# A projected block and a group's row transposes move into the attention's third place, in a decoder layer

## The chip, the cores and the metric

The kernel runs on one core of one Trainium2 chip. The metric is the device time in microseconds (us) of one execution, the median of several runs. Engines are named as in the profile: PE (TensorE, the matmuls), PEld (its weight loads), DVE (VectorE), ACT (ScalarE), POOL (GpSimd) and SP (the queue that issues most transfers).

## The reference

Four sequences of 512 rows and 512 columns go through one decoder layer, in float32:

```python
x = x + attn(layernorm(x))           # causal, 16 heads of 32, with q, k, v, o weights and biases
x = x + xattn(layernorm(x), ctx)     # no weights; q = layernorm(x), k = v = ctx; masked scores are -10000
x = x + relu(h @ W_up.T) @ W_down.T + sum(softmax(top2(h @ W_gate.T))) * (h @ W_expert)   # h = layernorm(x)
```

Both attentions subtract the largest score of each row before the exponential. In the cross attention a masked score is -10000 and not minus infinity, so rows whose largest score lies far below take part with their masked columns too; the kernel adds these from sums over the columns behind the diagonal.

## The kernel before

The loop over the four sequences `b` runs in program order; the engines' orders are the order in which the Python code records the instructions (a manual schedule for PE, DVE, ACT and POOL). Semaphores and PSUM buffers are set by the framework. PSUM holds four tiles of tag "ps", each a pair of 512-column banks (`pair`); a new tile takes a buffer that was freed, and its first matmul waits for the engine that read it last.

An attention has 16 heads in four groups `g` of four (HG = 4, 32 rows each) and works in two stages.

- `with_maxima` (L905) goes through ten units of scores, two row blocks or one at a time: `maxima` computes scores of 128 queries by up to 512 keys (tiles `sm_`, four heads side by side in row tiles of 32), ACT copies them to SBUF (`s_`), POOL masks the diagonal (L312), DVE takes the negated row maxima (`nm_`, L324). Between the units PE gets full-array matmuls from a list of `steps` (`fill`), spread evenly by `due`: projections of this or a neighbouring sequence. When a group's maxima are complete, `split` (L341) writes each as three bfloat16 parts into `parts0` or `parts1`. `rows` (L352) transposes these on PE with four 128x128 matmuls into rows `mrow_`, for groups 0 and 1 within this stage.
- `attend` (L954) goes through ten units of transposed scores (`scores`, tiles `sc_`, two pairs each, the first for two heads and the second for the other two). A second set of matmuls (L416) adds the negated maxima from `mrow_`. ACT takes the exponential (`pt_`, or `sum_` for a group's first block), POOL masks the diagonal (L447), and `values` multiplies with v two units later (`pv_`, column tiles of 32, L482). Row sums are made partly by DVE, which adds the later blocks onto `sum_` (`add_up`, L552), and one matmul with ones at the end (`summed`, L558).

Before, groups 2 and 3 of a self-attention get their row transposes together behind unit 3 of `attend` (`mt_s_both`, eight transposes, counted from unit 0). In a cross-attention group 2's stand at the end of `with_maxima`, group 3's behind unit 3, with group 2's broadcast of the maxima over heads (`masked_sums`, L374); group 3's broadcast stands behind unit 7.

The steps that fill `with_maxima` are the query and key projections (`query_key`, ACT adds the bias), the value projection (`value`, DVE adds the bias, L685), `up` (ACT takes the relu), `gate`, `down` (DVE adds to x, L843) and `expert` (DVE weighs and adds, L867). Each projects one block of 128 rows or columns with four matmuls; two blocks share one PSUM pair, which is read once both are done:

```python
if t % 2 == 0:
    made[0] = pair(f"pm_v{b}_{t}")
yield from project(made[0][:, t % 2, :], e.xn_t, wv_sb, t)
if t % 2 == 1:
    nc.vector.tensor_tensor(e.v[:, t - 1 : t + 1, :], made[0], ..., ALU.add)
```

The attentions are named s0 to s3 and c0 to c3. The fill of s0 is the rest of its query and key projections and its value projection; that of s1 and s2 the previous sequence's up, gate and down; that of s3 four experts and two ups; that of c1 query and key of the next sequence and four experts.

Of the kernel before, what the change touches and what calls it, by code (L numbers as in the profile page):

```python
# [18 lines left out]
P = 128  # L19
# [7 lines left out]
def decoder_layer(  # L27
# [37 lines left out]
    def pair(name):  # L65

        return ps.tile([P, 2, S], F32, tag="ps", name=name)


    def load_x(b):  # L70
        xb = act.tile([P, NT, D], F32, tag="x", name=f"x_{b}", bufs=2)
# [194 lines left out]
    class Attention:  # L266
# [82 lines left out]
            nc.vector.tensor_copy(pt[:, :, :, 1], rest)  # L349
            nc.vector.tensor_tensor(pt[:, :, :, 2], rest, pt[:, :, :, 1], ALU.subtract)  # L350

        def rows(self, g, both=None, half=0):  # L352


            if both is None:
                tp = ps.tile([P, NT, P], BF16, tag="ps", name=f"mt_{self.name}_{g}")
            else:
                bank = both[:, 0, :].bitcast(BF16)
                tp = bank[:, half * S : (half + 1) * S].rearrange("p (i q) -> p i q", q=P)
            for i in range(NT):  # L360
                nc.tensor.transpose(tp[:, i, :], parts[g % 2][:, i, :], identb)
            self.mrow[g] = work.tile(
                [P, S], BF16, tag="mrow", name=f"mrow_{self.name}_{g}", bufs=4
            )

            def copy(engine=nc.vector.tensor_copy):
                engine(self.mrow[g], tp.rearrange("p i q -> p (i q)"))

            return [copy]

        def masked_sums(self, g, both=None):

            bc = (pair(f"mb_{self.name}_{g}") if both is None else both)[:, 1, :]
            nc.tensor.matmul(bc, lhsT=same, rhs=self.mrow[g], start=True, stop=True)  # L374
            return g, bc

        def masked(self, g, bc):
# [298 lines left out]
    def value(e):  # L676
        b, made = e.b, {}
        e.v = act.tile([P, NT, D], F32, tag="v", name=f"v_{b}")

        def one(t):  # L680
            if t % 2 == 0:
                made[0] = pair(f"pm_v{b}_{t}")
            yield from project(made[0][:, t % 2, :], e.xn_t, wv_sb, t)
            if t % 2 == 1:
                nc.vector.tensor_tensor(  # L685
                    e.v[:, t - 1 : t + 1, :],
                    made[0],
                    bv_sb.unsqueeze(1).to_broadcast([P, 2, D]),
                    ALU.add,
                )  # L690

        return [(lambda t=t: one(t)) for t in range(NT)]

    def context(e):

# [82 lines left out]
    def ffn(e):  # L778
        b, f_t, made = e.b, e.f_t, {}

        def up(f):
            if f == 0:
                made["h"] = act.tile(
                    [P, NC, S], F32, tag="o_t" if b != B - 2 else "f_t", name=f"hT_{b}"
                )
            if f % 2 == 0:
                made["u"] = pair(f"pm_u{b}_{f}")
            yield from project_t(made["u"][:, f % 2, :], wup_sb, f_t, f)
            if f % 2 == 1:
                nc.scalar.activation(made["h"][:, f - 1 : f + 1, :], made["u"], AF.Relu)  # L790
# [41 lines left out]
            nc.vector.tensor_reduce(made["rw"], ew, axis=AX.X, op=ALU.add)  # L832

        def down(t):
            if t % 2 == 0:
                made["d"] = pair(f"pm_d{b}_{t}")
            yield from project(made["d"][:, t % 2, :], made["h"], wdown_sb, t)
            if t == NT - 1 and b == B - 2:
                for n in range(2):
                    aside(f"d{b}_{n}", t - 1 + n, made["d"][:, n, :])  # L840
            elif t % 2 == 1:
                both = e.x[:, t - 1 : t + 1, :]
                nc.vector.tensor_tensor(both, made["d"], both, ALU.add)  # L843

        def expert(t):
            if b == B - 1 and t == NT - 1:
                yield from expert_parts(t)
                return
            last = b == B - 1 and t == NT - 2
            if t % 2 == 0:  # L850
                made["e"] = pair(f"pm_e{b}_{t}")
            yield from project(made["e"][:, t % 2, :], f_t, wexp_sb, t)
            for n in (0,) if last else (0, 1) if t % 2 == 1 else ():
                u = t - t % 2 + n
                weigh(u, made["e"][:, n, :], slice(0, D), nc.sync)
# [46 lines left out]
            yield from step() or ()  # L902
            yield

    def with_maxima(steps, a, first=0, norms=()):  # L905


        norms = list(norms)
        run(steps[:first])
        fill = matmuls(steps[first:])  # L910
        total = sum(1 if step.__name__ in ("share", "gate") else NC for step in steps[first:])

        units = []
        for g in range(0, NC, 2):
            units += [[(g, 1), (g + 1, 1)]]
            units += [u for k in (g, g + 1) for u in ([(k, 2), (k, 0)], [(k, NT - 1)])]

        lead = 2 if first else 0
        for _ in range(lead):
            next(fill)  # L920
        done, due, jobs, late = lead, float(lead), [], {3: NC - 1}
        todo = []
        for n, pieces in enumerate(units):
            new = a.maxima(pieces)
            if todo:
                todo.pop()(nc.gpsimd)
            if norms and n % 2 == 0:
                new.append(norms.pop(0))
            due += (total - lead) / len(units)

            count = round(due) - done
            for k in range(count):
                next(fill, None)
                done += 1
                if k == min(1, count - 1) and n in (5, 7):
                    jobs = a.rows((n - 5) // 2) + jobs
                if k == min(1, count - 1) and a.cross and n in (6, 8):
                    todo.append(a.masked(*a.masked_sums((n - 6) // 2)))
                if n == len(units) - 1 and k == count - (2 if count > 4 else 1):
                    if total >= 2 * len(units):  # L940
                        if a.cross:
                            a.rows(2)[0](nc.scalar.copy)
                    else:
                        late = {3: 2, 5: NC - 1}
                run(jobs[:1])
                jobs = jobs[1:]
            run(jobs)
            jobs = new
        for _ in fill:
            pass  # L950
        run(jobs)
        return late

    def attend(a, late):  # L954


        units = []
        for g in range(0, NC, 2):
            units += [[(g, 0)], [(g, 3), (g, 1)], [(g, 2), (g + 1, 2)]]
            units += [[(g + 1, 0)], [(g + 1, 3), (g + 1, 1)]]  # L960
        waiting, held, todo = [], [], []

        def values():
            made = waiting.pop(0)
            a.values(made)

            if len(made) > 1 and made[0][1] == 2:
                held.append(made[1:])
            elif waiting and waiting[0][0][1] > 0:
                if made[0][1] == 0 and held:  # L970
                    a.add_up(held.pop())
                a.add_up(waiting[0] if waiting[0][0][1] == 3 else waiting[0][:1])
                if waiting[0][0][1] == 2 and waiting[0][1][0] == a.joined:
                    a.join(waiting[0][1], waiting[1][0])

        for n, pieces in enumerate(units):
            waiting.append(a.scores(pieces))
            if n in late:
                two = a.cross and late[n] == NC - 1
                together = not a.cross and len(late) == 1  # L980
                both = pair(f"mt_{a.name}_both") if two or together else None
                copies = a.rows(2, both, 1) if together else []
                copies += a.rows(late[n], both)

                more = [a.masked_sums(2, both)] if two else []
                for copy in copies:
                    copy(nc.scalar.copy)
                todo.extend(a.masked(*each) for each in more)
            if a.cross and n == 7:
                todo.append(a.masked(*a.masked_sums(3)))  # L990
            if n in (4 if a.joined is None else 6, 6, 9) and todo:
                todo.pop(0)()
            if n in (3, 4) and put_off:
                put_off.pop(0)()
            if len(waiting) > 2:
                values()
        while waiting:
            values()

    with tc.manual_schedule(engines=BY_HAND):  # L1000
# [11 lines left out]
        for b in range(B):  # L1012
# [2 lines left out]
            norms, turns = [], []  # L1015
            if more:
                after, norms, turns = norm_in(b + 1)
            late = with_maxima(between_self, sa, skip, norms)
            if b == B - 1:
                e.x = load_x(b)  # L1020
            attend(sa, late)
            if b > 0:
                add_bias(e)
            made = out_projection(e, sa, context(e) + turns)
# [4 lines left out]
            norm_cross(e, made, 2)  # L1029
            ca = Attention(e.cq_t, e.ck_t, e.cv, True, f"c{b}")  # L1030
            ca.e, ca.out = e, e.beh_t
            late = with_maxima(steps[3:], ca)
            if b + 2 < B:
                after.x = load_x(b + 1)
            attend(ca, late)
            if more:
                cvs[b + 1] = load_cv(b + 1)
            filler = value(after) if more else ahead
# [73 lines left out]
```

## Time and profile before

| | |
|---|---|
| median of 3 runs | 804.19 us (804.04 to 805.84) |
| profiled execution, span from first to last instruction | 803.7 us |
| mean granted TensorE clock in it | 0.998 |
| PE busy, matmuls | 794.0 us, 99%, 5588 records |
| DVE busy | 565.9 us, 70% |
| ACT busy | 395.2 us, 49% |
| POOL busy | 339.6 us, 42% |

The span of the profiled execution lies 0.5 us below the median of the runs; what lies around the span is not in the profile. A float32 matmul stands as two records in it, a bfloat16 matmul as one. "Idle before" names what ended an engine's idle time. A matmul's end is modelled, so that a short wait can stand within busy time; starts of instructions are better compared than their durations.

### The profile page before, as it was taken

What the parts mean: (1) busy time and instruction counts of PE and PEld (TensorE: products, weight loads), DVE (VectorE), ACT (ScalarE), POOL (GpSimd) and SP (SyncE); (2) the same over time, 40 slices, a digit from 0 to 9 for tenths busy, and PEclk for the clock granted to TensorE, in tenths of its full rate; (3) what the DMA queues carried; (4) which work ended last, traced back from release to release, by engine and by line L of the source; (5) the groups of instructions that cost most, each with busy time, mean ns of one, the idle gap of its engine ahead of it and who ended that gap; (6) DMA issues with size and microseconds to landing.
All of it is one profiled execution on the core that took longest, in us unless ns stands there. A gap on an engine that the chain in (4) does not pass through costs nothing.

```text
span 803.7 us, 13927 instructions
## 1 busy us (share of the span) xinstructions
PE 794.0 (99%) x5588; PEld 378.9 (47%) x5592; DVE 565.9 (70%) x963; ACT 395.2 (49%) x448; POOL 339.6 (42%) x523
## 2 busy tenths in 40 slices
PE   8999999999999999999999999999999999999998
PEld 6444454444444454444544455444444444444544
DVE  2378855889679854678867786588959766988512
ACT  2457516871456615567055742687156833674110
POOL 3434612564234732257332482256423652475100
PEclk9999999999999999999999999999999999999999
DMA  9710000001010000021100000000102000000101
GB/s 301 275 28 1 2 1 1 2 27 54 1 27 2 2 0 1 2 78 55 53 14 14 1 2 0 1 1 2 53 28 80 2 1 1 1 2 1 53 1 52
DMA packets 15282, 24.51 MB, mean 30 GB/s; under 512 B 2033, under 2 KB 5361, under 8 KB 15217
## 3 DMA queue, kind: packets, MB, share of 16 engines
q1 hardware_dynamic: 14496, 22.96, 8.6%
q8 instruction: 44, 0.72, 0.4%
q10 hardware_dynamic: 720, 0.66, 0.2%
q14 instruction: 22, 0.17, 0.1%
HBM read 19.42 MB, written 4.19 MB: 29 GB/s over the span
## 4 chain that ended last, share of the span: by engine, by line
PE 95%; ACT 2%; issue 1%; DMA 1%; DVE 0%; ACTq 0%
PE pm_qk L241 14%; PE pm_d L229 7%; PE pm_u L241 7%; PE pm_v L229 7%; PE pm_o L725 7%; PE pm_e L229 7%; PE pv_c L482 6%; PE pv_s L482 6%; PE sm_c L293 6%; PE sm_s L293 6%; PE sc_s L405 5%; PE sc_c L405 5%; PE sc_s L416 1%; PE sc_c L416 1%; PE tp_a L255 1%
## 5 line engine op out<-in xcount | busy, mean ns | idle before, releaser
L324 DVE TENSOR_REDUCE nm_s<-s_s 128x2 f32<-128x1024 f32 (+3 forms) x128 | 96.9, 810 | 34.7 <-POOL s_s L312 34.7
L324 DVE TENSOR_REDUCE nm_c<-s_c 128x2 f32<-128x1024 f32 (+3 forms) x128 | 95.8, 810 | 31.0 <-POOL s_c L312 31.0
L304 ACT COPY s_s<-sm_s 128x1024 f32<-128x1024 f32 x80 | 77.1, 1015 | 70.7 <-PE sm_s L293 36.7
L304 ACT COPY s_c<-sm_c 128x1024 f32<-128x1024 f32 x80 | 77.1, 1016 | 35.9 <-PE sm_c L293 16.2
L312 POOL TENSOR_SCALAR_AFFINE_SELECT s_c<-s_c 128x512 f32<-128x512 f32 (+1 forms) x80 | 43.9, 550 | 100.4 <-ACT s_c L304 100.4
L312 POOL TENSOR_SCALAR_AFFINE_SELECT s_s<-s_s 128x512 f32<-128x512 f32 (+1 forms) x80 | 43.8, 551 | 94.4 <-ACT s_s L304 94.4
L552 DVE TENSOR_TENSOR sum_s<-sum_s,pt_s 128x256 f32<-128x256 f32 (+2 forms) x72 | 59.9, 897 | 15.4 <-PE pv_s L482 15.4
L439 ACT ACTIVATE pt_c<-sc_c 128x1024 f32<-128x1024 f32 x64 | 61.7, 1031 | 18.1 <-PE sc_c L416 10.1
L447 POOL TENSOR_SCALAR_AFFINE_SELECT pt_c<-pt_c 128x512 f32<-128x512 f32 (+1 forms) x64 | 52.9, 833 | 20.7 <-ACT pt_c L439 20.2
L229 PE MATMUL pm_d<-wdown_sb,hT 128*128 128x512 f32 x128 | 61.5, 611 | 0.0
L241 PE MATMUL pm_qk<-xnT,wk_sb 128*128 128x512 f32 x128 | 61.0, 606 | 0.0
L241 PE MATMUL pm_u<-fT,wup_sb 128*128 128x512 f32 x128 | 59.3, 605 | 0.0
L439 ACT ACTIVATE pt_s<-sc_s 128x1024 f32<-128x1024 f32 x56 | 53.9, 1030 | 10.5 <-POOL pt_s L447 5.5
L229 PE MATMUL pm_v<-wv_sb,xnT 128*128 128x512 f32 x128 | 58.8, 600 | 0.0
L725 PE MATMUL pm_o<-wo_sb,oT_s 128*128 128x512 f32 x128 | 57.8, 596 | 0.0
L405 PE MATMUL sc_c<-cqT,ckT 32*128 32x384 f32 (+3 forms) x512 | 56.4, 464 | 0.9 <-ACT sum_c L439 0.9
L241 PE MATMUL pm_qk<-xnT,wq_sb 128*128 128x512 f32 x120 | 56.7, 605 | 0.0
L229 PE MATMUL pm_e<-wexp_sb,fT 128*128 128x512 f32 x120 | 56.3, 604 | 0.0
L447 POOL TENSOR_SCALAR_AFFINE_SELECT pt_s<-pt_s 128x512 f32<-128x512 f32 (+1 forms) x56 | 48.0, 865 | 16.9 <-ACT pt_s L439 16.2
L405 PE MATMUL sc_s<-qT,kT 32*128 32x128 f32 (+3 forms) x512 | 54.1, 464 | 0.9 <-ACT sum_s L439 0.9
L293 PE MATMUL sm_c<-ckT,cqT 32*128 32x512 f32 (+3 forms) x512 | 47.5, 460 | 0.0
L293 PE MATMUL sm_s<-kT,qT 32*128 32x512 f32 (+3 forms) x512 | 47.0, 461 | 0.0
(171 smaller groups left out, 1268.1 us busy)
## 6 DMA issues: line engine op xcount, KB each, us to landing
cv<-in_ctx_dram SPq DMA_DIRECT2D x16, 256.0 KB, 4.4
out_dram<-x SPq DMA_DIRECT2D x15, 256.0 KB, 2.0
xin<-in_x_dram SPq DMA_DIRECT2D x12, 256.0 KB, 2.8
x<-in_x_dram SPq DMA_DIRECT2D x12, 256.0 KB, 4.2
wq_sb<-in_wq_dram SPq DMA_DIRECT2D x2, 512.0 KB, 6.7
wk_sb<-in_wk_dram SPq DMA_DIRECT2D x2, 512.0 KB, 7.7
wv_sb<-in_wv_dram SPq DMA_DIRECT2D x1, 1024.0 KB, 7.8
wo_sb<-in_wo_dram SPq DMA_DIRECT2D x1, 1024.0 KB, 9.5
```

The source lines that it names most:

```text
L229: nc.tensor.matmul(pm, lhsT=lhs_t[:, c, t * P : (t + 1) * P], rhs=w[:, c, :], start=(c == 0), stop=(c == NC - 1),)
L241: nc.tensor.matmul(pm, lhsT=w[:, c, f * P : (f + 1) * P], rhs=rhs_t[:, c, :], start=(c == 0), stop=(c == NC - 1),)
L293: nc.tensor.matmul(scs[r // 2][:, r % 2, c : c + (i + 1) * P], lhsT=self.q_t[h, g, i * P : (i + 1) * P], rhs=self.k_t[h, g, : (i + 1) * P] ...
L304: nc.scalar.copy(s, scs[n])
L312: nc.gpsimd.affine_select(out=diagonal, in_=diagonal, compare_op=ALU.is_ge, fill=NEG, base=0, pattern=[[0, 2], [0, len(pieces)], [-1, P]], ...
L324: nc.vector.tensor_reduce(self.nm[g][:, i, 2 * n : 2 * n + 2], made[n][:, :, c : c + (i + 1) * P], axis=AX.X, op=ALU.max, negate=True,)
L405: nc.tensor.matmul(scs[r // 2][:, r % 2, c : c + S - j * P], lhsT=self.k_t[h, g, j * P : (j + 1) * P], rhs=self.q_t[h, g, j * P :], start= ...
L439: nc.scalar.activation(pt, scs[n], AF.Exp)
L447: nc.gpsimd.affine_select(out=diagonal, in_=diagonal, compare_op=ALU.is_ge, fill=0.0, base=0, pattern=[[0, 2], [0, len(pieces)], [1, P]], ...
L482: nc.tensor.matmul(pv[r * HD : (r + 1) * HD, u, j * P :], lhsT=ones if u else self.v[:, j, h * HD : (h + 1) * HD], rhs=pts[r // 2][:, r % ...
L552: nc.vector.tensor_tensor(to, to, pts[n][:, :, c : c + S - j * P], ALU.add)
L725: nc.tensor.matmul(pms[t // 2][:, t % 2, :], lhsT=a.out[:, c, t * P : (t + 1) * P], rhs=wo_sb[:, c, :], start=(c == 0), stop=(c == NC - 1),)
```

## The change

In s0 to s3 and in c1, the last step of the fill is taken out of `with_maxima` and kept. In `attend`, behind unit 1, come three of its four matmuls, then group 2's four row transposes into the other bank of the same PSUM pair (in c1: group 2's broadcast), then its fourth matmul. The last two maxima jobs of DVE (one reduction and the split of group 3) are recorded behind the block's evacuation. Group 3's row transposes go behind unit 5's values. There they are sixteen matmuls of 128 rows by 32 columns, one for each of four heads and four row blocks, in a PSUM pair of their own, in place of four of 128 by 128; c1's broadcast of group 3 is four column tiles. To have a block alone, the last two blocks of these fills (the first two of up in s3) get a PSUM pair and an evacuation each. In s0 six matmuls of the fill, not two, stand ahead of the first unit, and value blocks go in the order 0, 1, 3, 2. The due times of the fill are counted without the kept step.

```diff
+    latest = {}
+    def block(name):
+        latest["block"] = pair(name)
+        return latest["block"][:, 0, :]
...
-        def rows(self, g, both=None, half=0):
+        def rows(self, g, both=None, half=0, bank=0, columns=False):
+            if columns:
+                tp = (pair(f"mt_{self.name}_{g}") if both is None else both)[:, half, :]
+                tp = tp.rearrange("p (i q) -> p i q", q=P)
+                for i in range(NT):
+                    for r in range(HG):
+                        nc.tensor.matmul(
+                            tp[r * HD : (r + 1) * HD, i, :],
+                            lhsT=parts[g % 2][:, i, r * HD : (r + 1) * HD],
+                            rhs=identb, start=True, stop=True,
+                        )
...
-        def masked_sums(self, g, both=None):
+        def masked_sums(self, g, both=None, columns=False):
             bc = (pair(f"mb_{self.name}_{g}") if both is None else both)[:, 1, :]
-            nc.tensor.matmul(bc, lhsT=same, rhs=self.mrow[g], start=True, stop=True)
+            for r in range(HG if columns else 1):
+                h = slice(r * HD, (r + 1) * HD) if columns else slice(0, P)
+                nc.tensor.matmul(bc[h, :], lhsT=same[:, h], rhs=self.mrow[g], start=True, stop=True)
...
         def one(t):
+            if b == 0 and t >= NT - 2:
+                pm = block(f"pm_v{b}_{t}")
+                yield from project(pm, e.xn_t, wv_sb, t)
+                nc.vector.tensor_tensor(e.v[:, t, :], pm, bv_sb, ALU.add)
+                return
...
-        return [(lambda t=t: one(t)) for t in range(NT)]
+        order = (0, 1, 3, 2) if b == 0 else range(NT)
+        return [(lambda t=t: one(t)) for t in order]
...
-    def with_maxima(steps, a, first=0, norms=()):
+    def with_maxima(steps, a, keep, first=0, norms=()):
         run(steps[:first])
+        kept = matmuls(steps[-1:]) if keep else None
+        early = sum(1 if s.__name__ in ("share", "gate") else NC for s in steps[first:])
+        steps = steps[: len(steps) - 1] if keep else steps
...
-        lead = 2 if first else 0
+        lead = 6 if first else 0
...
+        if keep:
+            late = {5: NC - 1}
...
-        run(jobs)
-        return late
+        if not keep:
+            run(jobs)
+            jobs = []
+        return late, kept, jobs
...
+            if kept and n == 1:
+                for _ in range(NC - 1):
+                    next(kept)
+                run(jobs[:1])
+                if a.cross:
+                    bc = a.masked_sums(2, latest["block"])
+                else:
+                    copies = a.rows(2, latest["block"], bank=1)
+                for _ in kept:
+                    pass
+                if a.cross:
+                    todo.append(a.masked(*bc))
+                else:
+                    copies[0](nc.scalar.copy)
+                run(jobs[1:])
             if len(waiting) > 2:
                 values()
+            if kept and n in late:
+                a.rows(late[n], columns=True)[0](nc.scalar.copy)
+            if kept and a.cross and n == 7:
+                todo.append(a.masked(*a.masked_sums(3, columns=True)))
...
-            late = with_maxima(between_self, sa, skip, norms)
+            rest = with_maxima(between_self, sa, True, skip, norms)
...
-            late = with_maxima(steps[3:], ca)
+            rest = with_maxima(steps[3:], ca, b == 1)
```

`up`, `down` and `expert` get the same branch as `one` above: `up` for b = 2 and blocks 0 and 1 (ACT evacuates), `down` for b = 0 and 1 and blocks 2 and 3, `expert` for b = 0 and blocks 2 and 3.

More of the change, by code (lines that the diff above doesn't have):

```diff
@@ L350, in split @@
             nc.vector.tensor_tensor(pt[:, :, :, 2], rest, pt[:, :, :, 1], ALU.subtract)
-        def rows(self, g, both=None, half=0):
-            if both is None:
+        def rows(self, g, both=None, half=0, bank=0, columns=False):
[7 more added lines that the diff above has]
+                            lhsT=parts[g % 2][:, i, r * HD : (r + 1) * HD],
+                            rhs=identb,
+                            start=True,
+                            stop=True,
+                        )
+            elif both is None:
                 tp = ps.tile([P, NT, P], BF16, tag="ps", name=f"mt_{self.name}_{g}")
             else:
-                bank = both[:, 0, :].bitcast(BF16)
+                bank = both[:, bank, :].bitcast(BF16)
                 tp = bank[:, half * S : (half + 1) * S].rearrange("p (i q) -> p i q", q=P)
-            for i in range(NT):
+            for i in range(NT if not columns else 0):
                 nc.tensor.transpose(tp[:, i, :], parts[g % 2][:, i, :], identb)
@@ L369, in rows @@
             return [copy]
-        def masked_sums(self, g, both=None):
+        def masked_sums(self, g, both=None, columns=False):
             bc = (pair(f"mb_{self.name}_{g}") if both is None else both)[:, 1, :]
-            nc.tensor.matmul(bc, lhsT=same, rhs=self.mrow[g], start=True, stop=True)
+            for r in range(HG if columns else 1):
+                h = slice(r * HD, (r + 1) * HD) if columns else slice(0, P)
+                nc.tensor.matmul(
+                    bc[h, :], lhsT=same[:, h], rhs=self.mrow[g], start=True, stop=True
+                )
             return g, bc
@@ L785, in up @@
                 )
+            if b == B - 2 and f < 2:
+                pm = block(f"pm_u{b}_{f}")
+                yield from project_t(pm, wup_sb, f_t, f)
+                nc.scalar.activation(made["h"][:, f, :], pm, AF.Relu)
+                return
             if f % 2 == 0:
@@ L834, in down @@
         def down(t):
+            if t >= NT - 2 and b < B - 2:
+                pm = block(f"pm_d{b}_{t}")
+                yield from project(pm, made["h"], wdown_sb, t)
+                nc.vector.tensor_tensor(e.x[:, t, :], pm, e.x[:, t, :], ALU.add)
+                return
             if t % 2 == 0:
@@ L847, in expert @@
                 yield from expert_parts(t)
+                return
+            if b == 0 and t >= NT - 2:
+                pm = block(f"pm_e{b}_{t}")
+                yield from project(pm, f_t, wexp_sb, t)
+                weigh(t, pm, slice(0, D), nc.sync)
                 return
@@ L916, in with_maxima @@
             units += [u for k in (g, g + 1) for u in ([(k, 2), (k, 0)], [(k, NT - 1)])]
-        lead = 2 if first else 0
+        early = early >= 2 * len(units)
+        lead = 6 if first else 0
         for _ in range(lead):
@@ L921, in with_maxima @@
         done, due, jobs, late = lead, float(lead), [], {3: NC - 1}
+        if keep:
+            late = {5: NC - 1}
+        elif not early:
+            late = {3: 2, 5: NC - 1}
         todo = []
@@ L939, in with_maxima @@
                 if n == len(units) - 1 and k == count - (2 if count > 4 else 1):
[L940 to L944, printed above, removed]
+                    if early and a.cross:
+                        a.rows(2)[0](nc.scalar.copy)
                 run(jobs[:1])
@@ L950, in with_maxima, with attend @@
             pass
-        run(jobs)
-        return late
-    def attend(a, late):
+        if not keep:
+            run(jobs)
+            jobs = []
+        return late, kept, jobs
+    def attend(a, late, kept, jobs):
         units = []
@@ L977, in attend @@
             waiting.append(a.scores(pieces))
-            if n in late:
+            if n in late and not kept:
                 two = a.cross and late[n] == NC - 1
@@ L988, in attend @@
                 todo.extend(a.masked(*each) for each in more)
-            if a.cross and n == 7:
+            if a.cross and n == 7 and not kept:
                 todo.append(a.masked(*a.masked_sums(3)))
@@ L1017, in decoder_layer @@
                 after, norms, turns = norm_in(b + 1)
-            late = with_maxima(between_self, sa, skip, norms)
+            rest = with_maxima(between_self, sa, True, skip, norms)
             if b == B - 1:
                 e.x = load_x(b)
-            attend(sa, late)
+            attend(sa, *rest)
             if b > 0:
@@ L1031, in decoder_layer @@
             ca.e, ca.out = e, e.beh_t
-            late = with_maxima(steps[3:], ca)
+            rest = with_maxima(steps[3:], ca, b == 1)
             if b + 2 < B:
                 after.x = load_x(b + 1)
-            attend(ca, late)
+            attend(ca, *rest)
             if more:
```

## The prediction

> **What bounds the kernel now.** I read the page, then TensorE's waits, then the timelines of TensorE, VectorE and ScalarE over the first self-attention (s0).
>
> ```profile
> PE 794.0 (99%) x5588; PEld 378.9 (47%) x5592; DVE 565.9 (70%) x963; ACT 395.2 (49%) x448; POOL 339.6 (42%) x523
> ...
> PE 95%; ACT 2%; issue 1%; DMA 1%; DVE 0%; ACTq 0%
> ```
>
> The end is TensorE's queue, at a granted clock of 0.998. A microsecond counts only if TensorE's order loses or gains it. The view of its waits is nearly empty:
>
> ```profile
> PE sc_s L405 <- ACT sum_s L439: 0.9, 4, 0.2
> ```
>
> Busy time hides more, because a matmul's end is modelled. So I compare starts of the same unit of scores in two places. "Unit n" is the n-th set of scores in `attend`, from 0.
>
> ```profile
> 66.70 1.14 PE L405 MATMUL sc_s<-qT,kT 32*128 32x512 f32 x8
> ...
> 67.88 1.35 PE L405 MATMUL sc_s<-qT,kT 32*128 32x128 f32 x16
> ...
> 69.16 0.70 PE L405 MATMUL sc_s<-qT,kT 32*128 32x256 f32 x4
> 70.07 0.92 PE L405 MATMUL sc_s<-qT,kT 32*128 32x256 f32 x10 [0.21 <-ACT sum_s L439]
> ...
> 71.35 1.07 PE L482 MATMUL pv_s<-sum_s,v 128*32 128x512 f32 x8
> 72.35 1.17 PE L405 MATMUL sc_s<-qT,kT 32*128 32x512 f32 x6
> ...
> 74.10 0.62 PE L361 MATMUL mt_s_both<-identb,parts 128*128 128x128 bf16 x8
> 74.65 1.07 PE L482 MATMUL pv_s<-pt_s,v 128*32 128x128 f32 x16
> 75.65 1.50 PE L405 MATMUL sc_s<-qT,kT 32*128 32x128 f32 x16
> ...
> 78.18 1.16 PE L558 MATMUL pv_s<-sum_s,ones 128*32 128x512 f32 x8
> 79.28 1.14 PE L405 MATMUL sc_s<-qT,kT 32*128 32x512 f32 x8
> ...
> 81.56 1.31 PE L405 MATMUL sc_s<-qT,kT 32*128 32x128 f32 x16
> ```
>
> Unit 2 lasts from 69.16 to 71.35, 2.19; its twin, unit 7, takes 1.38 (84.02 to 85.40). Unit 3 takes 1.75 (72.35 to 74.10), its twin, unit 5, 1.29. Unit 4 takes 1.64, unit 9 1.50. So 0.81 + 0.46 + 0.14 = 1.4 us of each attention are waits for ScalarE's exponentials to free PSUM. All eight attentions show the first two within 0.15.
>
> **The change on TensorE alone.** A float32 512-column matmul stands as two records of 0.427, so 0.853. The moved block is four, 3.41, out of the maxima stage and into the attention: no work less.
> Added: a full-array run between row-tiled ones costs 0.21 (three matmuls take 2.77, not 2.56); with four bfloat16 transposes inside, another 0.28 (3.05, as from 47.98 to 51.03, where four transposes stand inside three matmuls). Block 3.41 + 0.21 + 0.28 = 3.90; unit 1, now followed by another mode, 1.37 for 1.28.
> Removed: the eight transposes, 74.65 - 74.10 = 0.55.
> From the attention's start to L558, before: 78.18 - 66.70 = 11.48, and 3.41 in the maxima: 14.89. After: units and values 1.18 + 1.37 + 3.90 + 1.38 + 1.00 + 1.29 + 1.00 + 1.50 + 0.89 = 13.51. TensorE alone gains 1.38 an attention. Now its waits, from the built order and its semaphores.
>
> **Wait 1: unit 1 on VectorE.** VectorE is loaded while TensorE fills:
>
> ```profile
> 50.23 0.42 DVE L367 COPY mrow_s<-mt_s 128x512 bf16<-128x512 bf16 x1 [3.32 <-PE mt_s L361]
> ...
> 57.12 1.22 DVE L685 TENSOR_TENSOR v<-pm_v,bv_sb 128x1024 f32<-128x1024 f32 x1 [0.81 <-PE pm_v L229]
> ...
> 65.53 1.26 DVE L324 TENSOR_REDUCE nm_s<-s_s 128x2 f32<-128x768 f32 x2
> 66.81 1.23 DVE L685 TENSOR_TENSOR v<-pm_v,bv_sb 128x1024 f32<-128x1024 f32 x1
> ```
>
> From 50.23 to 66.81 it idles 0.81 in all. The maxima stage loses 3.41 of TensorE's work but none of VectorE's, and unit 1's second pair of heads now needs the PSUM pair that VectorE frees with the add of the single block (`pm_v_3`; `pm_d_2` in s1 and s2). Queued before that add: all reductions but group 3's last five (s0) or four (s1, s2), the splits of groups 0 to 2, two row copies, the next layer norm.
> In s0 something comes first. `lead` 6 puts the first maxima unit 3.41 later but spreads the rest thinner, so unit (1,3) starts at 43.76, not 42.93, and ScalarE's query and key come 0.83 later:
>
> ```profile
> 46.61 0.68 ACT L648 ACTIVATE qT<-pm_qk,bqs_sb 128x512 f32<-128x512 f32 x1
> ```
>
> They end at 48.12. The next unit starts at 46.73 and needs them 0.51 in: 0.9 lost (now 0.13). `mt_0` slips to 50.67, VectorE's copy to 51.1. VectorE's list then lasts 66.81 - 50.23 - 0.81 (the idle goes, the add is behind a reduction) - 0.42 (one reduction later) + 0.68 (half add) = 16.0: done at 67.1. TensorE starts the attention at 66.70 - 3.41 + 0.87 = 64.15 and wants the buffer 1.23 in, at 65.4: it waits 1.75.
> In s1 (s2 is its copy) TensorE loses two stalls that the changed fill removes, 0.31 and 0.24 (units at 219.29 and 241.15). It starts at 249.94 - 3.41 - 0.55 = 245.98 and wants the buffer at 247.2. VectorE does one reduction and one row copy ahead of the gate instead of behind it, and so stands at 232.05 where it stood at 233.55; from there 15.2 without idle to group 3's second reduction (248.74 before), and the half add 0.68: 247.95, 0.8 late.
> In s3 there is no layer norm to make; but the fill's `pm_u_0` waits for the two weighings of `pm_e_2`, now behind five reductions more: VectorE from 598.95, without idle, comes to 613.4 (before 611.86, and 2.7 of reductions moved in front, 1.2 moved away). TensorE is there after eight units of 2.985, two sets of transposes (0.45) and a ninth unit of scores (1.08) from 586.94: 612.35. So 1.05 late. c1: 0.3 in the maxima (unit (2,3) on query and key), none in unit 1.
>
> **Wait 2: the row sums on VectorE.** L558 needs the six adds of L552. Behind the block VectorE has its evacuation 0.7, a reduction 1.2, the split 1.0 to 1.6 (73.67 - 72.16 = 1.5), the adds 4.6: 7.8 to 8.1 after the block's end. TensorE needs 1.38 + 1.00 + 1.29 + 1.00 + 1.50 + 0.89 = 7.06 and 0.11 to the second pair: 0.6 late in s0, s1, s2. In c1 adds of 5.0 and a longer split (1.9): 1.4 late. In s3 no evacuation stands there and the adds start at the first values: 0.25, and 0.2 on unit 3.
>
> **Wait 3: unit 6 on ScalarE.** The fourth group's transposes take the PSUM pair that unit 6 used, so unit 6's second heads need the second exponential of unit 5, not the first:
>
> ```profile
> 80.66 1.94 ACT L439 ACTIVATE sum_s<-sc_s 128x1024 f32<-128x1024 f32 x2 [0.98 <-PE sc_s L416]
> ```
>
> That ends at 82.60, 3.33 after unit 5's start. Before, the second heads began 2.46 after it (81.73). So 0.9 an attention, four times; the transposes lie under it. In c1 unit 5 and the joint sums take long enough; there the transposes cost their own time.
> That time has no row. Four full transposes take 0.22; four 128-column float32 column tiles 0.11, so sixteen at most 0.46. I take 0.27, nearest the bfloat16 row, and 0.22 to 0.46 as ends. c1's broadcast in column tiles (0.21 for 0.32) saves nothing: unit 8 waits for ScalarE anyway (2.10 for 1.29).
>
> The Trainium skill, TensorEngine Tiling (Array Packing), Restrictions, says that column tiling disables the fast weight load, and that speaks against sixteen small loads in place of four. No run here shows bfloat16 column tiles; loads of 0.109 (the 128x32 row) one behind another would make 1.74, 0.85 over wait 3 in four attentions and 1.5 in c1, by estimate 814 in all.
>
> **Sum**, each attention to L558's end, then unit 6:
> - s0: TensorE -1.38 + 0.87 + 1.75, sums +0.5 (0.6, of which the 0.11 stall there goes): +1.7; unit 6 +0.9: +2.6.
> - s1, s2: -1.38 - 0.55 + 0.8 + 0.5 = -0.6; +0.9: +0.3 each.
> - s3: -1.38 + 1.05 + 0.45 = +0.1; +0.9: +1.0.
> - c1: -1.38 + 0.3 + 1.4 = +0.3; +0.27: +0.6.
> Together 2.6 + 0.6 + 1.0 + 0.6 = +4.8 on the profiled span of 803.7; the median of the runs, 804.19, is 0.5 more, which lies around the span. 803.7 + 4.8 + 0.5 = 809.0.
> POOL and SP keep their order; no DMA is added.
>
> **Rivals.**
> *Faster: VectorE keeps up.* If it frees the buffer by 65.4 in s0 and 247.2 in s1, has the sums in time, and no unit of the maxima waits, only wait 3 stays: 4 x (-1.38 + 0.9) - 1.1 (s1, s2) - 1.38 + 0.27 (c1) = -4.1: 800.1. It decides once VectorE is 0.8 to 1.75 us earlier than I count. For it: VectorE idles 5.2 before the gate in s1. Against: behind it there is no idle. Chance 0.10.
> *No change to speak of.* VectorE half as late as counted, waits for ScalarE in full: s0 -1.38 + 0.87 + 0.87 + 0.25 + 0.9 = +1.5; s1, s2 -0.4 each; s3 +0.25; c1 -0.25. +0.7, so 804.9. Within 0.3% (2.4 us, about what a measurement of this kernel can tell from no change): 0.20. For it: 0.4 us on a list of 16 is a small error.
> *Waits 1 to 3 as counted:* 809.0, chance 0.60.
> *Slower still.* Each VectorE list 0.6 longer at five places, where POOL works beside it (two casts of a split take 0.46 and 0.66 there, 0.20 elsewhere), and splits 0.3 longer in four: +4.2, 813.2. Chance 0.10.
>
> Range: low, VectorE 0.7 earlier at unit 1 of s0, s1, s2 and in s3's fill (2.8) and no wait for sums (0.5 + 0.5 + 0.5 + 0.25 + 1.4 = 3.15): 803.0; high 813.2. Faster by over 0.3% 0.10, within 0.20, slower 0.70.
>
> **What would show it.** Unit 2 at 1.4 and unit 3 near 1.3, so the old waits gone: right in every case. A wait for VectorE at unit 1 of 1.75 in s0 and 0.8 in s1 and s2; L558's second pair held by VectorE; unit 6 near 2.1, behind its transposes; in s0's maxima the unit (2,1) at 2.1 for 1.2. If unit 1 takes 1.4 in all, VectorE keeps up and I am wrong towards 800.

## The result, and the profile after

The changed kernel takes 808.42 us (median of 6 runs, 807.22 to 809.67), the kernel before 804.14 (804.04 to 805.84): a ratio of 1.0049, 95% interval 1.0036 to 1.0062. It is slower by 4.3 us; forecast were 4.8. Three of the changed kernel's six runs have a mean clock of 0.998 and are its slowest (809.1 to 809.7); by their times two of the six of before are of that kind, and the medians of the others, 807.55 and 804.07, lie 3.5 apart.

The two profiled executions do not start alike, so their spans cannot be subtracted. The views of TensorE's clock by stretch (from:to, length, busy time and records, granted clock, DMA share, GB/s), of before and then of after:

```profile
9.00:10.00 1.00, 1.00 (x7) 0.50 1.08 380
```

```profile
9.00:10.00 1.00, 1.00 (x10) 1.00 1.05 369
```

Before, TensorE ran at half clock from about 8.5 to 11.9 us, and its first query projection starts at 11.97; after, it starts at 10.28. From there to the end of the last matmul it is 788.53 before and 792.58 after: +4.05. All changes "from the start" below are measured so, against the changed kernel where nothing else is said. They are good to 0.1: the first ten records of the projections take 2.16 before and 2.26 after, and where a run starts late they are the shorter ones again.

The page of after, engines and chain:

```profile
PE 793.1 (98%) x5655; PEld 373.6 (46%) x5655; DVE 564.1 (70%) x966; ACT 396.6 (49%) x449; POOL 338.1 (42%) x523
...
PE 86%; DVE 9%; ACT 3%; issue 1%; DMA 1%; POOL 0%; ACTq 0%
```

TensorE is busy 0.9 less in a longer span, and VectorE, which had no share of the chain, carries 9% of it. TensorE's waits (in total, times, longest) name the places:

```profile
PE sc_s L428 <- DVE v L707: 1.5, 1, 1.5
PE sc_s L428 <- ACT sum_s L462: 1.5, 4, 0.4
...
PE pm_u L248 <- DVE x L911: 1.4, 1, 1.4
PE sc_s L428 <- DVE x L872: 0.7, 2, 0.4
...
PE sm_s L300 <- ACT qT L671: 0.5, 1, 0.5
```

In this order: unit 1 of s0, unit 6 of the four self-attentions, the fill of s3, unit 1 of s1 and s2, the maxima unit (2,1) of s0. Part of each wait stands within busy time, so the sizes come from starts. TensorE's timeline over s0:

```profile
62.44 1.14 PE L428 MATMUL sc_s<-qT,kT 32*128 32x512 f32 x8
...
63.62 0.39 PE L428 MATMUL sc_s<-qT,kT 32*128 32x128 f32 x4
65.53 1.14 PE L428 MATMUL sc_s<-qT,kT 32*128 32x128 f32 x12 [1.52 <-DVE v L707]
...
66.81 2.84 PE L236 MATMUL pm_v<-wv_sb,xnT 128*128 128x512 f32 x6
...
70.72 1.15 PE L428 MATMUL sc_s<-qT,kT 32*128 32x256 f32 x16
...
72.02 1.06 PE L505 MATMUL pv_s<-sum_s,v 128*32 128x512 f32 x8
...
77.89 1.65 PE L581 MATMUL pv_s<-sum_s,ones 128*32 128x512 f32 x8
79.47 1.14 PE L428 MATMUL sc_s<-qT,kT 32*128 32x512 f32 x8
...
82.84 1.14 PE L428 MATMUL sc_s<-qT,kT 32*128 32x128 f32 x12 [0.38 <-ACT sum_s L462]
...
84.13 1.07 PE L505 MATMUL pv_s<-pt_s,v 128*32 128x128 f32 x16
```

And over units 0 and 1 of s3:

```profile
619.88 1.14 PE L428 MATMUL sc_s<-qT,kT 32*128 32x512 f32 x8
...
621.06 1.05 PE L428 MATMUL sc_s<-qT,kT 32*128 32x128 f32 x16
...
622.34 2.84 PE L248 MATMUL pm_u<-fT,wup_sb 128*128 128x512 f32 x6
```

The old stall of unit 2 is gone: it takes 1.30 (70.72 to 72.02), 2.19 before. Unit 1 takes 3.19 (63.62 to 66.81), 1.9 longer than in s3, where nothing holds it (1.28); the sums at 77.89 take 1.58, those of the next group 0.97; and from unit 5's start to the values behind unit 6 it is 4.66 (79.47 to 84.13), 3.74 before.

By attention, between the places where TensorE begins the last sums (`ls_s`) of a self-attention or the transposes behind c1; in s0 that is 94.17 before and 95.19 after, and the 1.69 of the start:

| | s0 | s1 | c1 | s2 | s3 | sum |
|---|---|---|---|---|---|---|
| forecast | +2.6 | +0.3 | +0.6 | +0.3 | +1.0 | +4.8 |
| measured | +2.7 | +0.15 | -0.2 | +0.15 | +1.2 | +4.0 |

### The profile page after: what moved, and what is told of

Read it like the earlier page. It is cut to its first block, busy times and chain, and to the rows that moved or that the text cites. A ratio compares the mean times of both kernels' runs of the same rounds, so it can differ in the third digit from the quotient of the medians.

```text
span 806.1 us, 14068 instructions
## 1 busy us (share of the span) xinstructions
PE 793.1 (98%) x5655; PEld 373.6 (46%) x5655; DVE 564.1 (70%) x966; ACT 396.6 (49%) x449; POOL 338.1 (42%) x523
## 4 chain that ended last, share of the span: by engine, by line
PE 86%; DVE 9%; ACT 3%; issue 1%; DMA 1%; POOL 0%; ACTq 0%
PE pm_qk L248 13%; PE pm_u L248 7%; PE pm_o L754 7%; PE pv_c L505 6%; PE pm_v L236 6%; PE pm_e L236 6%; PE sm_c L300 6%; PE pv_s L505 5%; PE sc_s L428 5%; PE sc_c L428 5%; PE pm_d L236 5%; DVE nm_s L331 4%; PE sm_s L300 3%; PE sc_s L439 1%; PE pv_s L581 1%
## 5 line engine op out<-in xcount | busy, mean ns | idle before, releaser
L575 DVE TENSOR_TENSOR sum_s<-sum_s,pt_s 128x256 f32<-128x256 f32 (+2 forms) x72 | 57.8, 867 | 16.6 <-PE pv_s L505 16.6
L470 POOL TENSOR_SCALAR_AFFINE_SELECT pt_s<-pt_s 128x512 f32<-128x512 f32 (+1 forms) x56 | 45.5, 824 | 32.4 <-ACT pt_s L462 32.2
L428 PE MATMUL sc_s<-qT,kT 32*128 32x128 f32 (+3 forms) x512 | 50.8, 462 | 3.8 <-DVE v L707 1.5
```

The source lines that it names most:

```text
L428: nc.tensor.matmul(scs[r // 2][:, r % 2, c : c + S - j * P], lhsT=self.k_t[h, g, j * P : (j + 1) * P], rhs=self.q_t[h, g, j * P :], start= ...
L470: nc.gpsimd.affine_select(out=diagonal, in_=diagonal, compare_op=ALU.is_ge, fill=0.0, base=0, pattern=[[0, 2], [0, len(pieces)], [1, P]], ...
L575: nc.vector.tensor_tensor(to, to, pts[n][:, :, c : c + S - j * P], ALU.add)
```

## The experiments

All are the changed kernel with an edit, but for one, which is the kernel before with an edit. The theory is that of the prediction: VectorE gates unit 1 and the row sums, ScalarE unit 6. Its rivals were that TensorE's own new work is the loss, and that a wait taken away at one place comes back at the next.

### Unit 6: the place of the transposes

```diff
-            late = {5: NC - 1}
+            late = {5 if a.cross else 4: NC - 1}
```

> The changed kernel, but in the self-attentions group 3's sixteen row transposes stand behind unit 4's values (where the row sums lie between them and the next scores) instead of unit 5's; c1 keeps unit 5. Theory (wait 3 is the exponential of unit 5, and only the place makes it): units 5 and 6 and what lies between take 3.74 as before the change, not 4.66, and the transposes cost 0.34 behind unit 4: -0.58 in each of four attentions, -2.3, so 806.1. Rival (the sixteen small loads are the cost): they cost the same at the other place, 808.4. Wait 2 is untouched: the sums still stand 0.6 late.

805.14 us against 804.00 of before beside it (ratio 1.0011, 1.0003 to 1.0020). From the start -2.4, 0.6 in each self-attention. Unit 6 of s0, in TensorE's timeline, has no wait left in front of it:

```profile
80.54 1.07 PE L505 MATMUL pv_s<-sum_s,v 128*32 128x512 f32 x8
81.53 1.31 PE L428 MATMUL sc_s<-qT,kT 32*128 32x128 f32 x16
```

The place makes wait 3, as counted. And whether the sixteen tiles cost anything by themselves:

```diff
-                a.rows(late[n], columns=True)[0](nc.scalar.copy)
+                a.rows(late[n])[0](nc.scalar.copy)
```

> The changed kernel, but group 3's row transposes are four of 128 by 128, not sixteen column tiles, in the same place and in a PSUM pair of their own. Theory (sixteen cost 0.34 as the changed kernel's profile has them, four 0.22 and up to 0.1 for the change of mode, and in the self-attentions unit 6 waits for ScalarE whichever it is): no change within 0.2 each, 808.4. Rival (sixteen small weight loads are what is slow): 0.85 less in each of four attentions and 1.5 in c1, 803.5.

807.60 us (ratio 1.0039, 1.0025 to 1.0054); from the start within 0.1. The self-attentions are as they were, but for the 0.1 of the start in s0; unit 6 waits for ScalarE there whichever it is. c1, where the transposes cost their own time, is 0.1 longer with the four. Four full transposes, in its timeline, occupy TensorE from 83.25 to 83.58:

```profile
83.25 0.40 PE L380 MATMUL mt_s<-identb,parts 128*128 128x128 bf16 x4
83.58 0.49 PE L428 MATMUL sc_s<-qT,kT 32*128 32x128 f32 x4
```

That is 0.33, and the sixteen take 0.34 (81.64 to 81.98 in the changed kernel): the small weight loads, 81.64 to 81.87, lie under the matmuls. The restriction that the Trainium skill, TensorEngine Tiling (Array Packing), Restrictions, puts on column tiling costs nothing here, and the 814 worked out from it falls.

### Unit 1: what VectorE does ahead of the single block's add

```diff
+            if keep and n == len(units) - 1:
+                jobs, new = [], jobs + new
...
-                run(jobs[:1])
+                run(jobs[:-2])
...
-                run(jobs[1:])
+                run(jobs[-2:])
```

> The changed kernel, but VectorE's reductions for the ninth maxima unit (and the layer norm's last step there) are recorded in attend, ahead of the kept block's evacuation and behind the add of the single block that unit 1 waits for; before the kept block VectorE idles 2.3. Theory (unit 1 waits for whatever VectorE does ahead of that add): in s0 one reduction of 0.94 stands ahead no more, in s1 and s2 two of 0.64 each, more than the 0.65 waited there: -0.9, -0.65, -0.65 = -2.2, so 806.2; s3 and c1 as they are. Rival (the lateness is handed on to the row sums): the sums wait as much longer, 808.4.

805.31 us (ratio 1.0018, 1.0009 to 1.0027). From the start -2.4: s0 -0.9, s1 and s2 -0.8 each, s3 and c1 nothing. In s0 the add now ends at 64.79, and TensorE goes on at 64.85; VectorE's line, then TensorE's:

```profile
64.11 0.68 DVE L707 TENSOR_TENSOR v<-pm_v,bv_sb 128x512 f32<-128x512 f32 x1
```

```profile
64.85 1.14 PE L428 MATMUL sc_s<-qT,kT 32*128 32x128 f32 x12 [0.65 <-DVE v L707]
```

In s0 nearly all that is taken out ahead of the add is won (0.94), in s1 and s2 the whole wait is. Nothing came back at the sums; VectorE idles ahead of the block's evacuation, 2.3 in s0 of the changed kernel and still 1.4 here.

### The six matmuls ahead of s0's first unit

```diff
-        lead = 6 if first else 0
+        lead = 2 if first else 0
...
-            due += (total - lead) / len(units)
+            if first:
+                due += 3 if n < 5 else (total - 17) / 5
+            else:
+                due += total / len(units)
```

> The changed kernel, but in s0's maxima two matmuls stand ahead of the first unit, not six, then three in each of the first five units and eleven spread over the last five, so that unit (2,1) comes as far behind its query and key as before the change. Theory (the six ahead spread the rest so thin that this unit waits 0.9 for ScalarE): that wait goes, 0.9, and VectorE, whose list starts with the first group's transposes, starts about 1.3 earlier against the same work, so that unit 1 of s0 waits 0.4 less as well: -1.3, 807.1. Rival (VectorE's list is as late as ever, and TensorE only reaches unit 1 earlier): what is won in the maxima is waited at unit 1, 808.4.

806.93 us (ratio 1.0034, 1.0021 to 1.0047); from the start -0.8. The wait for query and key is gone from TensorE's list, and unit 1's wait for `v` stands at 1.5 as before. So the first half of the expectation held; the 0.4 at unit 1 did not come: VectorE's list was earlier by as much as TensorE, not by more.

### The row sums: three tries

The first moves the sums, so that VectorE has time:

```diff
-            if (first if g in self.added else js == {0}) and g - 1 in self.added:
+            if js == {0} and g - 1 in self.added:
```

> The changed kernel, but in the self-attentions group 0's row sums (L581 of the changed kernel) stand behind unit 3's values instead of at unit 2's. Theory (the sums wait for VectorE's adds, and unit 6 waits for ScalarE because the fourth group's transposes take its PSUM pair): the sums no longer wait, 0.6 in each of four attentions, 2.4; and they now lie between the scores of units 5 and 6, so that the exponential of unit 5 is done in time: 0.7 to 0.85 in each of four, about 3.1. Together -5.5 on the changed kernel's 808.4: 802.9. Rival (what is lost is TensorE's own work, mode changes and sixteen small transposes): no change, 808.4. Rival (VectorE's lateness is handed on to the next place): only unit 6's wait goes, -3.1, 805.3.

814.62 us (ratio 1.0128, 1.0111 to 1.0144), 5.7 slower from the start, where 5.5 faster was expected. The sums wait no more, but ScalarE does, in its timeline:

```profile
81.62 1.94 ACT L462 ACTIVATE sum_s<-sc_s 128x1024 f32<-128x1024 f32 x2 [2.84 <-PE pv_s L581]
```

Group 2's first exponential is written to the SBUF tile that holds group 0's sums (both have the tag `ck_t`). Until L581 has read it, unit 5's exponential cannot start, and unit 6 and the transposes wait for that. Neither theory nor rival had this; the sums stand as early as they do for the sake of this tile.

The second moves the values of unit 0, and the adds with them:

```diff
+                a.values(waiting.pop(0))
                 for _ in range(NC - 1):
                     next(kept)
                 run(jobs[:1])
...
-                run(jobs[1:])
+                a.add_up(waiting[0])
...
+            if kept and n == 3:
+                run(jobs[-2:])
```

> The changed kernel, but in the five attentions the values of unit 0 stand ahead of the kept block, not behind unit 2, the adds of unit 1's exponentials directly behind the block's evacuation on VectorE, and the last reduction and group 3's split behind unit 2's adds. Theory (the row sums wait only because VectorE's adds start too late): the adds start 2.3 earlier, and the 0.8 of s0, s1 and s2, 0.6 of s3 and 1.0 of c1 that unit 2's values and the sums are late go, -4.0. Unit 3 now follows unit 2 without values between them and may wait for the block's PSUM pair or ScalarE, up to 0.2 in each of five, +1.0. So -3.0 on 808.4: 805.4. Rival (POOL's masks of unit 2, not VectorE's place, end the adds): the sums are as late as they were, 808.4; with unit 3 waiting, 809.4.

815.32 us (ratio 1.0141, 1.0128 to 1.0154), 7.3 slower from the start. The sums' wait is gone in s0 (the values and sums take 0.89 and 0.97), but unit 3 follows unit 2 directly and needs the exponential of unit 2; TensorE's timeline:

```profile
74.08 1.75 PE L428 MATMUL sc_s<-qT,kT 32*128 32x512 f32 x6
...
76.41 1.07 PE L505 MATMUL pv_s<-pt_s,v 128*32 128x128 f32 x16
```

Unit 3 takes 2.33 (74.08 to 76.41), 1.51 in the changed kernel: +0.8, not the 0.2 allowed for. In c1, which loses 2.8, unit 5 waits as well. About as much is lost ahead of the block: unit 0's values need POOL's masks of its exponential. From unit 0 to the end of these values it is about 4.85 in s1, s2, s3 and c1; units 0 and 1 and the same values take 4.23 in s1 and s2 of the changed kernel and 3.46 in s3 and c1. In s0 nothing of this shows, because unit 1 still waits for `v` in front of them. Here a wait is handed on; unit 0's values between two units of scores are time that ScalarE and POOL need.

The third leaves TensorE's order alone:

```diff
-                run(jobs[:1])
+                run(jobs[:-1])
...
-                run(jobs[1:])
+                run(jobs[-1:])
```

> The changed kernel, but VectorE's last reduction of group 3 stands ahead of the kept block's evacuation, in the 2.3 to 3.5 in which VectorE idles there, not behind it; TensorE's order is unchanged. Theory (the row sums are late by what VectorE does between the evacuation and the adds): the adds start when unit 0's values have been read, 0.75 earlier in s0, s1 and s2 and 1.1 earlier in c1, and the sums, late by 0.8 and 1.0, by as much less; s3, where the adds start at the values already, is as it was: -0.75 x 3 - 1.0 = -3.2 on 808.4, 805.2. Rival (the adds end with POOL's mask of unit 2, whatever starts them): no change, 808.4.

806.42 us (ratio 1.0031, 1.0020 to 1.0041): from the start -1.2, of -3.2 expected; 0.2 in s0, s1 and s2 each, 0.5 in c1, and the 0.1 of the start. The adds do start 0.7 earlier, but end only 0.2 earlier. VectorE's lines of s0 here, and then in the run with the early values:

```profile
74.42 5.02 DVE L575 TENSOR_TENSOR sum_s<-sum_s,pt_s 128x256 f32<-128x256 f32 x6 [0.84 <-PE pv_s L505]
```

```profile
73.33 2.49 DVE L575 TENSOR_TENSOR sum_s<-sum_s,pt_s 128x256 f32<-128x256 f32 x4
...
76.34 1.70 DVE L575 TENSOR_TENSOR sum_s<-sum_s,pt_s 128x512 f32<-128x512 f32 x2 [0.53 <-POOL pt_s L470]
```

Six adds need 4.2 where POOL leaves the first four alone, 4.6 in the changed kernel, and 5.0 when they start together with POOL's masks of unit 2 (74.50 in this run). So the sums are late by the adds' own time between the end of unit 0's values and L581, and most of it cannot be moved away on VectorE's side.

### Together

The three edits that held (transposes behind unit 4, reductions behind the add, uneven fill):

> The changed kernel with three edits at once: the row transposes behind unit 4, the ninth unit's reductions behind the single block's add, and the uneven fill of s0. Theory (three causes in three places): their gains by their own traces add up, 2.4 + 2.4 + 0.8 = 5.6 on 808.4: 802.8. Rival (they are one chain, each gives the next wait): what the largest gave alone, 2.4 to 3, so 805.5 to 806.

802.45 us, ratio to before 0.9981 (0.9972 to 0.9990); from the start -5.6. The gains add up to the tenth: three causes in three places. With the early values on top and group 2's split behind the add:

> The three edits and the early values of unit 0 together; group 2's split of the self-attentions is also recorded behind the single block's add. Theory: 5.6 for the three, 3.0 for the values, and what is left of s0's wait at unit 1, 0.7, goes with the split: 808.4 - 9.3 = 799.1, below the kernel before. Rival (VectorE's list is full, and what is moved out of one wait comes back in the next): no better than the three, 802.8.

814.29 us (ratio 1.0123, 1.0110 to 1.0136): from the start 10.4 slower than the three edits, where the early values alone cost 7.3. The split did its part: no wait for `v` is left in TensorE's list. But unit 0's values now come upon POOL's masks in every self-attention. TensorE's wait for them, in the run with the early values alone and then here:

```profile
PE pv_s L505 <- POOL sum_s L470: 0.5, 1, 0.5
```

```profile
PE pv_s L505 <- POOL sum_s L470: 2.0, 4, 0.5
```

From unit 0 to the end of these values it is 4.85 in s1 and s2 again, so all that the late reductions had won there is lost. Here the rival was right that a wait comes back, though on POOL and not in VectorE's list. So the last version keeps the split and takes the earlier reduction instead; `with_maxima` is called with `more` for `True` in the self-attentions, which leaves s3 as before, and its two blocks of up share a pair again:

```diff
+            if keep and n == len(units) - 2 and not a.cross:
+                jobs, split = jobs[:-1], jobs[-1:]
             if keep and n == len(units) - 1:
-                jobs, new = [], jobs + new
+                jobs, new = [], split + jobs + new
...
-            rest = with_maxima(between_self, sa, True, skip, norms)
+            rest = with_maxima(between_self, sa, more, skip, norms)
```

> The three edits of the run three_moves, with the last reduction ahead of the evacuation, group 2's split of the self-attentions behind the single block's add, and s3 as in the kernel before (no kept block there). Theory: on 802.5, -0.75 x 3 - 1.0 for the sums, -0.9 for what s0 still waits at unit 1, and -0.6 for s3, whose own +1.2 the earlier transposes had brought to 0.6: 797.7. Rival (VectorE's list in s0 to s2 is full, so that the moved split and reduction delay the block's evacuation, and unit 3 waits for its PSUM pair): -0.6 and c1's -1.0 alone, 800.9.

799.18 us against 804.00, ratio 0.9935 (0.9921 to 0.9949): faster than both kernels; from the start -8.4 where -10.7 was expected. TensorE's list has left, of 9.3 us in the changed kernel:

```profile
PE warm L192 <- POOL ident masks.py:199: 1.5, 1, 1.5
PE tp_a L262 <- DVE xn_a L219: 1.3, 1, 1.3
PE sc_c L428 <- ACT sum_c L462: 0.6, 3, 0.2
PE sc_s L428 <- ACT sum_s L462: 0.2, 1, 0.2
```

The missing 2.3 lie mostly in the sums: the last reduction ahead of the evacuation was priced at 3.2 and is worth 1.1 alone.

### The start

In the kernel before, `keep_warm("warm", 12)` became `keep_warm("warm", 20)`.

> The kernel before with twenty warming matmuls at its start, not twelve. The profiled execution of before had a granted clock of 0.5 from 8.9 to 11.5 us, behind 2.4 us in which TensorE idled; the one of the changed kernel idled 1.4 and kept 1.0. Theory (the runs of one kernel differ by up to 2.4 us because the first transfers land at different times, and a long idle time at the start lowers the clock): with TensorE warm until about 8 no run shows the lower clock, all lie within 1 us, and the median stays near 803.8. Rival (the scatter has another cause): runs at 805 and above stay, one in four.

804.51 us (803.83 to 804.97, 11 runs) against 803.92 (803.59 to 805.63, 23 runs); ratio 1.0004, 0.9995 to 1.0012. All eleven had a mean clock of 1.0, and none is above 804.97; four of the 23 without the edit had 0.998, and they are the four highest, 805.4 to 805.6. The slower runs are those with the lower clock, and the profiles show that clock at the start. That the longer warming is what removed them is likely but not shown: by the rate of four in 23, eleven without one would still come about once in eight. The eleven spread over 1.1, and the median gains nothing: in the profile of this run the warming lasts until 8.9, and the first normalised rows were ready at 7.7.

## Why the prediction was right, and where it was not

The direction and the size came out of the three waits, and most terms stand:

- **TensorE alone.** The block with its transposes takes 3.91 in s0 (66.81 to 70.72); 3.90 was counted. Units 2 and 3 take 1.30 and 1.51; 1.38 and 1.29 were counted. The stall of unit 2 went; of unit 3's 0.46, 0.22 stayed, and it stands near 1.5 and not near 1.3, the sign that was to hold in every case. Unit 4 made up for it: 1.30, where 1.50 was counted.
- **Wait 1.** Unit 1 of s0, against s3's: 1.9, forecast 1.75; s1: 0.76 (2.04 for 1.28), forecast 0.8; the fill of s3: 1.4, forecast 1.05; the maxima unit (2,1) of s0: 0.82 longer than before (2.03 for 1.21), forecast 0.87. VectorE's list could be added up from the profile of before because it had almost no idle time in it. That it is the cause is shown by the late reductions for s0 to s2; for the fill of s3 it rests on the wait in TensorE's list.
- **Wait 2.** 0.8 late in s0 to s2, 0.6 in s3, 1.0 in c1; forecast 0.6, 0.25 and 1.4. The wait is there, its explanation was partly wrong. I counted a list behind the block (its terms add up to 7.5 to 8.1, not to 7.8 to 8.1), and in s0 the adds do start behind it. But without the reduction in it they start 0.7 earlier and end only 0.2 earlier: they start no earlier than unit 0's values end, and their length depends on POOL. In c1 split and adds took 1.4 and 4.6, where I had carried over the 1.9 and 5.0 of before; in s3 the adds took 5.0, as before, and unit 4's shorter time let TensorE arrive earlier.
- **Wait 3.** The stretch of units 5 and 6 grew by 0.92; forecast 0.9. Shown by the move of the transposes.
- **c1** was the term most off, +0.6 against -0.2: 0.4 of it the sums, 0.2 the transposes, whose stretch cost 0.09 and not 0.27, and 0.2 units of scores that ran faster than in s0's count.
- **Around the span.** I took 0.5 from the profiled 803.7 and the median 804.19. That execution was one with a half clock at its start, and runs of before take 2.1 more than their span (805.84 for 803.7); for the changed kernel it is 1.65. That the median came out only 0.6 below the forecast is in part luck: the sum was 0.8 too high, the 0.45 around the span was not foreseen, and the half clock at the start of more of the changed kernel's runs made 4.3 of the 3.5 that the others show.

The rival that VectorE keeps up fell with the wait of 1.5 at unit 1, the one that it is half as late with the sizes of wait 1. The slower one, lists made longer by POOL at five places, does not show in the row sums: six adds take 4.57 in s0 and 5.02 in s3, 4.57 and 5.04 before.

## What to carry to other kernels

Work moved on the bound engine is worth only what the engines behind it can follow: when TensorE loses filler, add up the other engine's list from its last idle time to the buffer that TensorE will want, and record ahead of that evacuation only what must be. A place in the order that looks free may pay for something else: a buffer that is read there (the sums), or time for other engines (the values between two units). Before two profiles are subtracted, look at how each one starts.

## What the hardware showed that was not expected

- **A VectorE add that starts while a POOL instruction runs waits for most of it.** Two rows of s0 in the changed kernel, VectorE's and POOL's:

```profile
74.53 1.38 DVE L575 TENSOR_TENSOR sum_s<-sum_s,pt_s 128x768 f32<-128x768 f32 x1
```

```profile
74.18 0.93 POOL L470 TENSOR_SCALAR_AFFINE_SELECT pt_s<-pt_s 128x512 f32<-128x512 f32 x1 [0.27 <-ACT pt_s L462]
```

  The add takes 0.94 where no POOL instruction runs at its start. Here the mask still has 0.58 to run, and the add is longer by 0.44. In 116 of the 120 adds of this trace the lengthening is, within 0.04, what the POOL instruction still had to run, less 0.14 (nothing where that is below 0). In the other four the mask is recorded 0.02 ahead of the add, and the mask is the longer one. An add of 128x256 takes 0.41 or up to 0.88, one of 128x768 up to 1.39 beside a mask and 2.03 beside POOL's TENSOR_TENSOR. The Trainium skill, SBUF — State Buffer, Who interferes with whom, says that a VectorE instruction with two SBUF inputs contends with a GpSimd one that reads SBUF and that the one issued later waits; these adds and masks are such a pair. The trace shows the wait; that its reason is the port that the page names is not shown by any run here.
- **Idle times of 1.9 to 2.4 us at the start were followed by a half clock, those of 1.0 to 1.7 were not** (one profiled execution each of twelve kernels, by their mean clocks of 0.997 and 0.998 against 0.999 and 1.0). The same skill's TensorE: Matmul & The Clock Gate, What's actually happening, has the clock fall after at least one idle window of about 3.4; here shorter ones sufficed. The half clock then stayed for 3.4, as from 8.5 to 11.9 in the run of before. What else decides it is open.
